# Pinned transposes and a moved projection in a fused attention layer, and joined square roots in the layer after it

## The chip, the core and the metric

The kernel is one program on one core of a Trainium2 chip. The metric is device time in microseconds (us) of one execution, as the median of several runs. A separate, profiled execution gives the trace. The engines are called PE (TensorE, with PEld for its weight loads), DVE (VectorE), ACT (ScalarE), POOL (GpSimd) and SP (which issues most DMAs).

## What is computed

Four layers, each a cross attention and a feed-forward network (FFN), run one after the other on x of shape (4, 256, 256) in float32, with a context of (4, 1601, 256). The change touches the attention of layer 2 and of layer 3 (layers are counted from 0). Cut to these:

```python
# layer 2: 16 query heads, 4 key heads, head size 128
x = layernorm(x)
q, k, v = heads(x @ wq), heads(x @ wk), heads(x @ wv)
q, k = rms_norm(q, q_norm_w), rms_norm(k, k_norm_w)
k_ctx, v_ctx = rms_norm(heads(ctx @ wk_ctx), k_norm_w), heads(ctx @ wv_ctx)
q, k = rotary(q), rotary(k)                      # the context's keys are not rotated
scores = q @ concat(k_ctx, k).T / sqrt(128) + causal_mask_on_the_tokens_part
x = x_in + concat_heads(softmax(scores) @ concat(v_ctx, v)) @ wo
# layer 3: 32 heads of size 8, keys of the context alone
x = layernorm(x)
q, k, v = heads(x @ Wq.T), heads(ctx @ Wk.T), heads(ctx @ Wv.T)
q, k = q * rsqrt(mean(q * q) + 1e-6), k * rsqrt(mean(k * k) + 1e-6)
x = x_in + concat_heads(softmax(q @ k.T / sqrt(8)) @ v)
x = x + quantized_ffn(layernorm(x))              # epsilon of both layer norms: 1e-5
```

## The kernel before

The program is written in a framework with a planner. The Python code gives the instructions in an order (the program order), the planner simulates the engines and puts each engine's instructions into a fixed sequence, in which an instruction that is ready in its simulation may go ahead of earlier ones. On the chip each engine follows that sequence. `tc.keep_in_program_order(ins)` puts `ins` behind the instruction that the code issued before it on the same engine; it holds back nothing else.

**Layer 2** (`l2_xattn`) works through 16 units (batch b, key head g); a unit has four query heads. Keys and values have 15 tiles of 128 rows: 12 of context, one of mixed rows (`CT` = 12), and two of tokens. The score of a query block of 32 is made with the query as weights in four column groups, so a score tile `s2` holds 4 x 32 partitions, and its softmax is made in parts: `scores` gives each partition a maximum `nm` and a sum `sm`, and exponentials `p`; `merge` transposes nm and sm (`ct`, `st`, tile `tm2`) on PE and works out one factor for each partition; `scale` multiplies p by it on POOL; `turn` transposes 32 x 32 blocks on DVE into `pT2`; `values` makes the value products into `o2`, which ACT copies into `at2`; `project` multiplies at by wo into `acc2`, and DVE adds it to x.

The main loop has two steps for each head, so steps 0 to 7 for each unit. In a step the program has scores of two chunks, a step of the softmax of the head before (`soft`), a half of the values of the head before that (`vals`), and then pieces of `prep`, which makes keys, values and queries of the next unit. The first units (`EARLY` = 5) take context keys made earlier from DRAM; the others make them here. The list `WHEN` says how many pieces each step takes; 17 in all for such a unit: two query products, eight pieces of key and value products (tiles 12 and 13; 14; 0 and 1; and so on up to 10 and 11), one that makes the roots and scales (`rstd`, L1031), two with query transposes (`tpqT`, L1048), four with key transposes (`tpk`, L1055). PSUM has two buffers for `s2` and two for the tag `tp`, which tpq, tpkv, tpqT, tpk and acc2 share.

The tokens' keys are rotated into `ko2` (L1024 to L1029) after all products, and scaled on POOL (L1042). The projection of a unit stands in step 3 of the next one, after that step's pieces, when the last values of its head 3 are done.

**Layer 3** works on one batch at a time, in eight groups of four heads. Scores of two context tiles go into two tiles `s3` of three, ACT makes exponentials `e3` (L1532), values follow one pair later. Beside this runs `beside`, a generator that is taken one step further with each pair: keys and values of the next batch (`l3_kv`, 13 tiles, squares, a root, scaling on POOL, transposes), its queries (`queries`) and the FFN of the batch before (`ffn`). Square roots are made on ACT in `rstd` (L72, L73), once for the layer norms of the next and of the previous batch (`norms`), once for the keys, once for the queries.

ACT loads another table (ACT_TABLE_LOAD) where the function changes between the square root and the exponential.

Of the kernel before, what the change touches and what calls it, by code (L numbers as in the profile page):

```python
# [51 lines left out]
class Kernel:  # L52
# [38 lines left out]
    def fill(self, n):  # L91

        for _ in range(n):
            next(self.early, None)
# [771 lines left out]
    def l2_xattn(self):  # L866
# [11 lines left out]
        with ExitStack() as es:  # L878
# [47 lines left out]
            def halves(ap):  # L926
                return ap.rearrange("p h (t d) -> p h t d", t=2)
# [15 lines left out]
            def prep(u, w, ctxT, res):  # L943
# [47 lines left out]
                for ms in ((12, 13), (14,), (0, 1), (2, 3), (4, 5), (6, 7), (8, 9), (10, 11)):  # L991
                    if early and ms[0] < CT:
                        continue
                    tp = ps.tile([P, 2, 256], F32, name="tpkv", tag="tp")
                    rows = P
                    for n, m in enumerate(ms):
                        for k in range(2):
                            if m < CT:
                                self.mm(tp[:, n, :], ctxT[:, k, m * P : (m + 1) * P], w["wkc"][:, k, :], k == 0, k == 1)
                            elif m == CT and early:  # L1000
                                pass
                            elif m == CT:
                                self.mm(tp[:96, n, :], ctxT[:, k, m * P : m * P + 96], w["wkc"][:, k, :], k == 0, k == 1)
                            else:
                                _, t0, rows = OWN[m - 13]
                                self.mm(tp[:rows, n, :], xb[:, k, t0 : t0 + rows], w["wks"][:, k, :], k == 0, k == 1)
                        if m == CT:
                            for k in range(2):
                                self.mm(tp[96:, n, :], xb[:, k, :32], w["wks"][:, k, :], k == 0, k == 1)
                    m, n = ms[0], len(ms)  # L1010
                    if m == CT and early:
                        for t, v in ((kr, tp[:, :, :HD2]), (va, tp[:, :, HD2:])):
                            nc.scalar.copy(t[96:, CT, :], v[96:, 0, :])
                            nc.scalar.copy(t[:, CT + 1, :], v[:, 1, :])
                    else:
                        nc.scalar.copy(kr[:rows, m : m + n, :], tp[:rows, :n, :HD2])
                        nc.scalar.copy(va[:rows, m : m + n, :], tp[:rows, :n, HD2:])
                    if rows < P:
                        nc.gpsimd.memset(kr[rows:, m, :], 0.0)
                    if m in (2, 6, 10, 14):  # L1020
                        squares(CT if m == 14 else m - 2, m + n)
                    yield
                ra, rb = tabs["l2_knw"]
                ko = one.tile([P, 3, HD2], F32, name="ko2")  # L1024
                t2 = one.tile([P, 3, HD2], F32, name="kt2")
                own = kr[:, CT:, :]
                nc.gpsimd.tensor_tensor(ko, own, ra, ALU.mult)
                nc.vector.tensor_tensor(halves(t2), swapped(own), halves(rb), ALU.mult)
                nc.gpsimd.tensor_tensor(ko, ko, t2, ALU.add)  # L1029
                m0 = CT if early else 0  # L1030
# [7 lines left out]
                for m in range(0, 0 if early else CT, 4):  # L1038
                    nc.gpsimd.tensor_tensor(
                        kr[:, m : m + 4, :], kr[:, m : m + 4, :], ss[:, m : m + 4, None].to_broadcast([P, 4, HD2]), ALU.mult  # L1040
                    )
                nc.gpsimd.tensor_tensor(ko, ko, ss[:, CT:NK, None].to_broadcast([P, 3, HD2]), ALU.mult)  # L1042
                yield
                qT = two.tile([P, 4, S], F32, name="qT2")
                for q in range(2):
                    tp = ps.tile([P, 4, P], F32, name="tpqT", tag="tp")
                    for h in range(4):
                        nc.tensor.transpose(tp[:, h, :], qo[q][:, h, :], self.ident)  # L1048
                    nc.scalar.copy(qT[:, :, q * P : (q + 1) * P], tp)
                    yield  # L1050
# [45 lines left out]
            def merge(nm, sm):  # L1096
# [3 lines left out]
                ct, st = t[:8, 0:P], t[:8, P : 2 * P]  # L1100
                nc.tensor.transpose(ct, nm, self.ident)
                nc.tensor.transpose(st, sm, self.ident)
                by = lambda ap: ap.rearrange("n (a j) -> n j a", a=4)
# [43 lines left out]
            def project(hd):  # L1147
                if hd["h"] < 3:
                    return
                b, at, wo = hd["b"], hd["at"], hd["wo"]  # L1150
# [42 lines left out]

            WHEN = [2, 2, 2, 2, 3, 0, 3, 3]
            WHEN_EARLY = [0, 1, 1, 2, 1, 0, 2, 1]
            soft, vals = None, None
            for n, (b, g) in enumerate(units):
                kT, va, qT = ready
                ready, pieces = [], None
                wo_now = wo  # L1200
                at = main.tile([P, 4, S], F32, name="at2", bufs=1)
                for h in range(4):
                    hd = {"nm": self.small.tile([P, 8], F32, name="nm2"), "sm": self.small.tile([P, 8], F32, name="sm2"),
                          "p": [], "va": va, "at": at, "h": h, "b": b, "wo": wo_now}
                    for c in (0, 2):
# [18 lines left out]
                        if pieces is not None:  # L1224
                            for _ in range((WHEN_EARLY if early else WHEN)[step]):
                                next(pieces, None)
                        if vals is not None and c == 2:
                            project(done)
                        if soft is not None and c == 0:
                            next(soft[0])  # L1230
                    done = soft[1] if soft is not None else None
                    vals = value_steps(soft[1]) if soft is not None else None
# [4 lines left out]
            for n in range(2):  # L1237
                next(soft[0])
                next(vals)
                if n == 0:  # L1240
                    next(soft[0])
            project(done)
            for _ in value_steps(soft[1]):
                pass
            project(soft[1])


# [27 lines left out]
    def l3_kv(self, b, st, early):  # L1275
# [6 lines left out]
        va = st["va"] = self.va3[b % 2]  # L1282
        ss = st["ss"] = self.a3.tile([P, (NM + 2) * NH3], F32, name="ss3")
        for m in range(NM):
# [16 lines left out]
            yield  # L1301
        nk = NM * NH3
        self.rstd(ss[:, :nk], ss[:, :nk], 1.0 / HD3, self.eps6)
        for m0, m1 in ((0, 4), (4, 8), (8, 12), (12, NM)):
# [30 lines left out]
    def l3(self, first):  # L1335
# [11 lines left out]
        with ExitStack() as es:  # L1347
# [10 lines left out]
            def bank():  # L1358
                return ps.tile([P, 512], F32, name="b3", tag="tp")

            def norms(bs):

                n = len(bs)
                mv = self.small.tile([P, n, 2, 2], F32, name=f"mv3{n}")
                rs = self.small.tile([P, n, 2], F32, name=f"rs3{n}")
                for t, b in enumerate(bs):
                    st = self.small.tile([P, 2, 6], F32, name="st3")
                    for q in range(2):
                        nc.vector.bn_stats(st[:, q, :], self.x[b][:, q, :])
                        nc.vector.bn_aggr(mv[:, t, q, :], st[:, q, :])  # L1370
                self.rstd(rs, mv[:, :, :, 1], 1.0, self.eps5)
                res = []
                for t, b in enumerate(bs):
                    xn = self.xn.tile([P, 2, D], F32, name="xn3", tag="xn")
                    for q in range(2):
                        nc.vector.tensor_scalar(
                            xn[:, q, :], self.x[b][:, q, :], mv[:, t, q, 0:1], rs[:, t, q : q + 1],
                            ALU.subtract, ALU.mult,
                        )
                    res.append(xn)  # L1380
                return res

            def queries(b, st, xn, fill=lambda n: None):

                ss = st["ss"]
                fill(0)
                tp = bank().rearrange("p (k q t) -> p k q t", k=2, q=2)
# [13 lines left out]
                self.l3_squares(st, qr, NM, True, one)  # L1401
                nk = NM * NH3
                self.rstd(ss[:, nk:], ss[:, nk:], 1.0 / HD3, self.eps6)
                qrv = qr.rearrange("p q (h d) -> p (q h) d", d=HD3)
                nc.vector.tensor_tensor(qrv, qrv, ss[:, nk:, None].to_broadcast([P, 2 * NH3, HD3]), ALU.mult)
                fill(2)
# [154 lines left out]
            def beside(b, st):  # L1561

                if b + 1 < B:
                    kv = st["kv"] if b == 0 else self.l3_kv(b + 1, st, lambda: False)
                    if b:
                        for _ in range(3):
                            next(kv)
                            yield
                    xns = norms([b + 1] + ([b - 1] if b else []))
                    for _ in range(NM - 3 if b else NM - sum(FIRST3)):  # L1570
                        next(kv)
                        yield
                    qs = queries(b + 1, st, xns[0])
                    for _ in range(2):
# [4 lines left out]
                    for _ in qs:  # L1579
                        yield  # L1580
                    old = xns[1:]
                else:
                    for _ in range(3):
                        yield
                    old = norms([b - 1])
                if b == 0:
# [12 lines left out]
            self.l2_add(0)  # L1599
            for _ in queries(0, first, norms([0])[0], lambda n: [next(kv) for _ in range(FIRST3[n])]):  # L1600
                pass
# [44 lines left out]

            xn = norms([B - 1])[0]
            tail = [ffn(B - 1, q, xn, wide) for q in range(2)]
# [157 lines left out]
```

## Time and profile before

| what | value |
|---|---|
| median of 3 runs | 2759.39 us (2759.36 to 2767.87) |
| the profiled execution's own time | 2769.84 us |
| its span, first to last instruction | 2768.1 us |
| mean granted PE clock | 0.979 of full speed |
| busy: PE, PEld, DVE, ACT, POOL | 2630.5, 1483.2, 1354.0, 1245.5, 679.7 us |
| ACT_TABLE_LOAD ahead of a root (L72) | 40, 1283 ns each |
| ACT_TABLE_LOAD ahead of layer 2's exponentials (L1090) | 19 |
| ACT_TABLE_LOAD ahead of layer 3's exponentials (L1532) | 11 |
| POOL, scaling of ko (L1042) | 16, 826 ns each |

A line of a timeline has the start, the length, the engine, the line of the code, the operation, the tile written and the tile read, the shape, the count, and in brackets the time that the engine stood idle before it with the instruction that ended the wait. Matrix products have all one line (L68), since a helper issues them; they are told apart by their tiles. A matrix product of float32 shows as two MATMUL records. The granted clock is the share of full speed at which PE was let run.

### The profile page before, as it was taken

What the parts mean: (1) busy time and instruction counts of PE and PEld (TensorE: products, weight loads), DVE (VectorE), ACT (ScalarE), POOL (GpSimd) and SP (SyncE); (2) the same over time, 40 slices, a digit from 0 to 9 for tenths busy, and PEclk for the clock granted to TensorE, in tenths of its full rate; (3) what the DMA queues carried; (4) which work ended last, traced back from release to release, by engine and by line L of the source; (5) the groups of instructions that cost most, each with busy time, mean ns of one, the idle gap of its engine ahead of it and who ended that gap; (6) DMA issues with size and microseconds to landing.
All of it is one profiled execution on the core that took longest, in us unless ns stands there. A gap on an engine that the chain in (4) does not pass through costs nothing. (4 is left out here: it accounts for less than half of the span.)

```text
span 2768.1 us, 43652 instructions
## 1 busy us (share of the span) xinstructions
PE 2630.5 (95%) x17377; PEld 1483.2 (54%) x17393; DVE 1354.0 (49%) x2604; ACT 1245.5 (45%) x2559; POOL 679.7 (25%) x916
## 2 busy tenths in 40 slices
PE   7999998998999999999999999998999999999997
PEld 4654446444555555555555656555555554544553
DVE  6421126125777766666666666765334323242323
ACT  2321114115444444444444444442325785766775
POOL 1012222214444343333433333432101001001000
PEclk9999999999999999999999999998999999999998
DMA  5133323333110000100001000001322000000000
GB/s 195 58 114 89 89 62 100 88 105 126 38 44 32 20 16 20 41 23 24 13 24 45 16 24 23 2 8 54 141 86 77 18 16 26 4 3 2 6 6 5
DMA packets 57140, 130.10 MB, mean 47 GB/s; under 512 B 7966, under 2 KB 27746, under 8 KB 55914
## 3 DMA queue, kind: packets, MB, share of 16 engines
q1 hardware_dynamic: 54352, 122.94, 13.8%
q8 instruction: 139, 2.28, 0.4%
q0 software_dynamic: 912, 2.49, 0.3%
q10 hardware_dynamic: 1674, 1.88, 0.2%
q14 instruction: 63, 0.52, 0.1%
HBM read 115.14 MB, written 12.14 MB: 46 GB/s over the span
## 5 line engine op out<-in xcount | busy, mean ns | idle before, releaser
L1090 ACT ACTIVATE p<-s,nm 128x448 f32<-128x448 f32 (+1 forms) x512 | 326.7, 644 | 436.2 <-DVE nm L1086 258.1
L1532 ACT ACTIVATE e<-s 128x1024 f32<-128x1024 f32 (+1 forms) x448 | 404.0, 960 | 152.8 <-PE s L68 147.8
L68 PE MATMUL s<-kT,qT 128*32 128x448 f32 (+1 forms) x4096 | 466.0, 566 | 3.9 <-ACT p L1090 3.8
L1126 POOL TENSOR_SCALAR p<-p,rm 128x448 f32<-128x448 f32 (+1 forms) x512 | 322.5, 651 | 554.2 <-DVE rm L1119 333.1
L68 PE MATMUL o<-pT,va 128*128 128x256 f32 (+2 forms) x1920 | 431.9, 376 | 4.4 <-DVE pT L1132 4.2
L68 PEld LDWEIGHTS o<-pT,va 128*128 128x128 f32 (+1 forms) x1920 | 345.5, 191 | 101.7 <-issue 60.2
L1132 DVE STREAM_TRANSPOSE pT<-p 128x896 f32<-128x896 f32 (+1 forms) x256 | 283.2, 1124 | 49.2 <-POOL p L1126 48.3
L68 PE MATMUL s<-qb,kT 32*128 32x256 f32 (+1 forms) x3328 | 272.9, 406 | 18.5 <-ACT e L1532 16.3
L1086 DVE TENSOR_REDUCE nm<-s 128x2 f32<-128x896 f32 (+1 forms) x256 | 282.6, 1105 | 3.5
L68 PEld LDWEIGHTS s<-kT,qT 128*32 128x32 f32 x4096 | 125.2, 111 | 243.7 <-issue 214.9
L68 PE MATMUL o<-e,va 128*32 128x256 f32 (+1 forms) x3328 | 238.2, 394 | 1.2 <-DVE os L1625 1.2
L68 PEld LDWEIGHTS s<-qb,kT 32*128 32x128 f32 (+1 forms) x3328 | 165.8, 182 | 113.1 <-issue 75.8
L68 PEld LDWEIGHTS o<-e,va 128*32 128x32 f32 (+1 forms) x3328 | 91.0, 110 | 115.6 <-issue 75.9
L380 DVE TENSOR_TENSOR f0h<-f0sg,f0u 128x512 f32<-128x512 f32 x48 | 33.0, 687 | 212.4 <-POOL f0sg L378 209.4
L68 PE MATMUL tpkv<-wkc,ctxT 128*128 128x256 f32 (+1 forms) x572 | 130.6, 379 | 0.0
L1559 POOL TENSOR_TENSOR x<-x,t 128x32 f32<-128x32 f32 x64 | 14.7, 250 | 471.9 <-DVE t L1554 471.9
L378 POOL TENSOR_TENSOR f0sg<-f0sg,f0gb 128x512 f32<-128x512 f32 x48 | 60.7, 1266 | 265.9 <-ACT f0sg L376 137.7
L1083 DVE TENSOR_TENSOR s<-s,mask 128x128 f32<-128x128 f32 (+1 forms) x256 | 82.7, 324 | 86.4 <-PE s L68 75.1
L376 ACT ACTIVATE f0sg<-f0g 128x512 f32<-128x512 f32 x48 | 28.7, 597 | 211.0 <-PE f0g L68 207.9
L68 PEld LDWEIGHTS tpkv<-wkc,ctxT 128*128 128x128 f32 (+1 forms) x572 | 107.5, 188 | 15.7
L1090 ACT ACTIVATION_READ_ACCUMULATOR p<-s,nm 128x1 f32 x512 | 100.9, 197 | 0.0
L68 PE MATMUL f0g<-xnT,wg 128*128 128x512 f32 x192 | 90.3, 593 | 0.7 <-ACT f0gT L65 0.7
(417 smaller groups left out, 3399.1 us busy)
## 6 DMA issues: line engine op xcount, KB each, us to landing
ctxT<-in_ctxT SPq DMA_DIRECT2D x10, 1664.0 KB, 8.3
wo<-in_l_wo SPq DMA_DIRECT2D x16, 512.0 KB, 3.6
wq<-in_l_wq SPq DMA_DIRECT2D x16, 512.0 KB, 3.5
f2wgu<-in_l_wgu SPq DMA_DIRECT2D x4, 2048.0 KB, 15.1
ctxn<-in_ctx SPq DMA_DIRECT2D x4, 1664.0 KB, 7.2
f0gb<-f0gd SPq DMA_DIRECT2D x16, 384.0 KB, 4.0
f0gb<-f0gd SPq DMA_DIRECT2D x16, 256.0 KB, 4.3
wks<-in_l_wks SPq DMA_DIRECT2D x16, 256.0 KB, 2.6
```

What stands on the lines that cost most here:

```text
L68: self.nc.tensor.matmul(out, lhsT, rhs, start=start, stop=stop, **kw)
L376: nc.scalar.activation(sg, pgt, AF.Silu)
L378: nc.gpsimd.tensor_tensor(sg, sg, gb[:, tb * 512 : (tb + 1) * 512], ALU.mult)
L380: nc.vector.tensor_tensor(h, sg, pu, ALU.mult)
L1083: nc.vector.tensor_tensor(sv, sv, mask[:, 2 * c : 2 * c + 2, : nt - CT, :].rearrange("p n t i -> p n (t i)"), ALU.add)
L1086: nc.vector.tensor_reduce(nm[:, 2 * c : 2 * c + 2], s[:, :, : nt * 32], AX.X, ALU.max, negate=True)
L1090: nc.scalar.activation(p[:, n, : nt * 32], s[:, n, : nt * 32], AF.Exp, bias=nm[:, e : e + 1], accum_out=sm[:, e : e + 1],)
L1126: nc.gpsimd.tensor_scalar(p[:, n, : nt * 32], p[:, n, : nt * 32], r[:, e : e + 1], 1.0, ALU.mult, ALU.mult)
L1132: nc.vector.transpose(pT[:, 2 * c : 2 * c + 2, :nt, :].rearrange("p n t i -> p n (t i)"), p[:, :, : nt * 32])
L1532: nc.scalar.activation(e[:kr, :, :n, :], s[t][:kr, :, :n, :], AF.Exp, scale=1.0 / math.sqrt(HD3))
L1559: nc.gpsimd.tensor_tensor(xt, xt, t[:, q], ALU.add)
```

## The change

In layer 2:

- the transposes of queries, of maxima and of sums are kept in program order;
- the rotation of the tokens' keys follows tile 14 in the program; its scaling moves from POOL to three activations on ACT;
- the projection of a unit is called in step 5 of the next unit (in step 3 before); for that `at2` has two buffers;
- `WHEN` takes one piece from step 4 to step 3.

In layer 3:

- layer norm statistics of batches 1 to 3 are made at once, at the start of batch 0's work beside;
- for batches 1 to 3 the roots of keys and queries, and the one for the layer norm of the previous batch's FFN, are one activation on one tile `ss3`, which has two more columns; the variance is entered there as 8 var + 8 (1e-5 - 1e-6), so that the root with scale 1/8 and bias 1e-6 gives that of var + 1e-5.

```diff
+                    if m == CT + 2:
+                        ra, rb = tabs["l2_knw"]
+                        ko = one.tile([P, 3, HD2], F32, name="ko2")
...
+                        nc.gpsimd.tensor_tensor(ko, own, ra, ALU.mult)
+                        nc.vector.tensor_tensor(halves(t2), swapped(own), halves(rb), ALU.mult)
+                        nc.gpsimd.tensor_tensor(ko, ko, t2, ALU.add)
                     if m in (2, 6, 10, 14):
                         squares(CT if m == 14 else m - 2, m + n)
                     yield
-                ra, rb = tabs["l2_knw"]
...
-                nc.gpsimd.tensor_tensor(ko, ko, t2, ALU.add)
...
-                nc.gpsimd.tensor_tensor(ko, ko, ss[:, CT:NK, None].to_broadcast([P, 3, HD2]), ALU.mult)
+                for m in range(3):
+                    nc.scalar.activation(ko[:, m, :], ko[:, m, :], AF.Copy, scale=ss[:, CT + m : CT + m + 1])
...
-                        nc.tensor.transpose(tp[:, h, :], qo[q][:, h, :], self.ident)
+                        tc.keep_in_program_order(nc.tensor.transpose(tp[:, h, :], qo[q][:, h, :], self.ident))
...
-                nc.tensor.transpose(ct, nm, self.ident)
-                nc.tensor.transpose(st, sm, self.ident)
+                tc.keep_in_program_order(nc.tensor.transpose(ct, nm, self.ident))
+                tc.keep_in_program_order(nc.tensor.transpose(st, sm, self.ident))
...
-            WHEN = [2, 2, 2, 2, 3, 0, 3, 3]
+            WHEN = [2, 2, 2, 3, 2, 0, 3, 3]
...
-                at = main.tile([P, 4, S], F32, name="at2", bufs=1)
+                at = main.tile([P, 4, S], F32, name="at2", bufs=2)
...
-                        if vals is not None and c == 2:
-                            project(done)
+                        if step == 5 and last is not None:
+                            project(last)
...
-        ss = st["ss"] = self.a3.tile([P, (NM + 2) * NH3], F32, name="ss3")
+        ss = st["ss"] = self.a3.tile([P, (NM + 2) * NH3 + 2], F32, name="ss3")
...
-        self.rstd(ss[:, :nk], ss[:, :nk], 1.0 / HD3, self.eps6)
+        if b == 0:
+            nk = NM * NH3
+            self.rstd(ss[:, :nk], ss[:, :nk], 1.0 / HD3, self.eps6)
...
+                if old is not None:
+                    stats(old)
+                    nc.vector.tensor_scalar(
+                        ss[:, nq:], mv[:, old, :, 1], float(HD3), HD3 * (1e-5 - 1e-6), ALU.mult, ALU.add
+                    )
+                elif b:
+                    nc.vector.memset(ss[:, nq:], 1.0)
+                xn = normed(b, rs[:, b, :])
...
-                self.rstd(ss[:, nk:], ss[:, nk:], 1.0 / HD3, self.eps6)
+                part = ss if b else ss[:, nk:nq]
+                nc.scalar.activation(part, part, AF.Sqrt, bias=self.eps6, scale=1.0 / HD3)
+                nc.vector.reciprocal(ss[:, nk : nq + 2 if b else nq], ss[:, nk : nq + 2 if b else nq])
...
+                if b:
+                    for c in range(0, nk, nk // 2):
+                        nc.vector.reciprocal(ss[:, c : c + nk // 2], ss[:, c : c + nk // 2])
...
-                    xns = norms([b + 1] + ([b - 1] if b else []))
+                    if b == 0:
+                        norms(range(1, B))
...
-                    qs = queries(b + 1, st, xns[0])
+                    qs = queries(b + 1, st, b - 1 if b else None)
...
-                    old = xns[1:]
+                    nq = (NM + 2) * NH3
+                    old = [normed(b - 1, st["ss"][:, nq:])] if b else []
```

Here `stats(b)` makes the layer norm statistics of one batch into `mv`, `normed(b, r)` subtracts the mean and multiplies by r, and `norms` does the statistics and one root for several batches. `nq` is the column behind the queries' sums.

## The prediction

> **What bounds the kernel now.** I read the profile in the order: busy time of each engine by stretch, who waits for whom on TensorE, timelines of the places named there. By the timelines, layer 2's attention runs from 658 to 1926 us (its units with keys made in the unit before, "full" units, from 950 on) and layer 3's from 2127 to 2742 us. Columns: stretch and its length, busy PE, PEld, DVE, ACT and POOL, granted clock, DMA:
>
> ```profile
> core 0: us, PE busy (x) PEld busy (x) DVE busy (x) ACT busy (x) POOL busy (x), PEclk, DMA share, GB/s
> 950.00:1905.00 955.00, 918.34 (x5735) 554.55 (x5734) 635.94 (x1048) 439.76 (x1183) 352.29 (x492) 0.99 0.07 21
> 2127.00:2742.00 615.00, 590.70 (x7105) 309.49 (x7118) 192.04 (x463) 445.24 (x497) 47.45 (x83) 0.98 0.04 12
> ```
>
> TensorE is busy 96% in both, the next engine 67% and 72%. Time can come only from PE's idle 36.7 and 24.3 us, and from clock that is not granted. The waits of PE in the first stretch (total us, times, longest):
>
> ```profile
> PE tpqT L1048 <- POOL qo L1035: 21.7, 22, 1.9
> PE tm L1102 <- ACT p L1090: 9.1, 12, 0.8
> PE tpk L1055 <- ACT kT L1057: 4.4, 11, 0.4
> ```
>
> These are the same three places in each of 11 units, as PE's timeline of one shows (start, length, what, idle before):
>
> ```profile
> 1314.91 3.29 PE L68 MATMUL o<-pT,va 128*128 128x256 f32 x14
> 1319.80 0.66 PE L1048 MATMUL tpqT<-ident,qo 128*128 128x128 f32 x4 [1.60 <-POOL qo L1035]
> 1320.80 0.66 PE L1048 MATMUL tpqT<-ident,qo 128*128 128x128 f32 x4 [0.34 <-POOL qo L1035]
> 1321.38 3.21 PE L68 MATMUL s<-kT,qT 128*32 128x448 f32 x32
> ...
> 1336.09 1.04 PE L1055 MATMUL tpk<-ident,kr 128*128 128x128 f32 x8
> 1336.97 0.27 PE L1101 MATMUL tm<-ident,nm 128*8 128x128 f32 x1
> 1338.02 0.27 PE L1102 MATMUL tm<-ident,sm 128*8 128x128 f32 x1 [0.78 <-ACT p L1090]
> 1338.68 0.52 PE L1055 MATMUL tpk<-ident,ko 128*128 128x128 f32 x3 [0.40 <-ACT kT L1057]
> ```
>
> The program writes the query transposes behind the score and value products of step 6; here they stand ahead of those scores (1321.38), where POOL is still scaling qo. The planner put them forward. Likewise the maxima's transposes (tm) stand ahead of the next unit's first scores.
>
> Layer 3 has one large wait, for exponentials, where ACT does a square root between two table loads:
>
> ```profile
> PE s L68 <- ACT e L1532: 16.3, 8, 2.6
> ```
>
> ```profile
> 2326.88 1.28 ACT L72 ACT_TABLE_LOAD   x1
> 2330.41 0.64 ACT L72 ACTIVATE ss<-ss,eps 128x416 f32<-128x416 f32 x1 [2.24 <-DVE ss L1330]
> 2331.07 1.28 ACT L1532 ACT_TABLE_LOAD   x1
> ```
>
> PE's next scores then come at 2333.43, after 2.61 idle. The eight waits: keys' roots 2.40, 2.61, 2.61; queries' roots 2.30 three times; norms 0.26 and 1.49.
>
> A wait costs more than its idle time. Two stretches with the same query stall:
>
> ```profile
> 984.00:990.00 6.00, 5.66 (x40) 2.14 (x40) 2.99 (x4) 2.78 (x9) 3.63 (x4) 0.72 0.01 3
> 1318.00:1324.00 6.00, 4.05 (x37) 1.77 (x40) 4.57 (x6) 4.67 (x12) 5.42 (x6) 1.00 0.01 3
> ```
>
> In the first the clock fell (0.72 over 6 us: 1.7 us lost), in the second not. Going through both layers in stretches of 2 us, I find six such falls in the full units, all behind a query stall, 1.7 each, **10.2 us**; in layer 3 they sum to **13.6 us**, all behind a root's wait.
>
> **What the Trainium skill says.** "TensorE: Matmul & The Clock Gate", section "Part 1: The HAM clock gate", says an idle PE falls to half clock and needs a busy window of about 3.4 us to recover, the window running freely. The trace agrees on the loss (half of 3.4 is the 1.7 seen) and on the chance in it (6 of 11 equal stalls), but 2 us of idle is enough here. "ScalarE: Activation LUTs", section "What ACT_TABLE_LOAD costs", gives 1.28 us a load plus 1.38 of drain; the trace has the 1.28, and the exponential starts right behind it. "PSUM — Partial Sum Buffer", section "Engine vs sequencer instructions": matmuls start in program order; so an early transpose holds all scores behind it, as above.
>
> **The change, part by part.**
>
> *Layer 2, pinned transposes.* tpqT goes behind step 6's 32 scores, two tm and 16 value products, 3.2+0.3+3.4 = 6.9 us of PE work. qo is ready at 1320.7; the transposes now could start at 1318.1. What is late next? The scores of step 6, which come forward into the gap: their first buffer is free only when the exponentials of step 5 have read it, 1319.97, the second at 1322.05 (ACT's timeline). That would put a stall of 1.8 in place of the 1.94. But the projection moves to step 5 (16 matmuls, 3.7 us in the trace at 1379.99; one DVE add of 0.69; no DMA), ahead of exactly these scores: first scores at about 1321.9, second half 1323.5. Cover holds by 1.9 and 1.4. So **-21.7** (bounds -21.7 and 0, if the projection lands elsewhere).
>
> *Clock.* Without a 2 us gap the six falls should go: -10.2; I leave one: **-8** (bounds -10.2 and 0).
>
> *Unit's end.* tm pinned behind the scores takes its wait of 0.78 away, but the third tpk there waits for a bank that ACT's kT copy at 1337.85 frees, and that copy stands behind the exponentials (until 1337.85). PE now waits for it from 1337.1 to about 1338.6: 1.4 for 1.18, as 0.25 of tm's work has left the gap. 11 x 0.25 = **+3** (bounds -13.5, if the planner finds filler, and +8, if the longer gap makes half of the units fall in clock at 1.7). tm runs some 5 us later at step 0; its reader on PE (L1117) today waits for query products till 1349.1 while DVE had it ready at 1341.4, so that costs nothing. Elsewhere tm already stands behind the scores.
>
> *Tokens' keys.* The two POOL and one DVE instruction of the rotation come earlier in the program, but in the trace all 16 already run straight behind ACT's copy of kr (1360.05): 0. On POOL 0.83 us a unit goes; POOL is 37% busy: 0. On ACT three 128x128 copies with a scale come in, not in the trace; the skill's price (the ScalarE section above: 186+0.83N ns, 93 a pointer, 93 overlapped) gives an estimate of 0.29 each; the trace's 128x512 kin takes 0.69, which that formula gives too. 0.9 us a unit, at ACT's busiest point, between the root and step 5's exponentials. Queued behind: those exponentials, and PE's step-6 scores behind them; the margins of 1.9 and 1.4 above cover it: **0** (bounds 0 and 11 x 0.9 = +10).
>
> *WHEN.* One key product (8 matmuls, 1.8 us, two copies) moves from step 4 to 3; a second buffer for at lets the projection wait two steps. PE work is the same: 0. No step moved past a queue issues a DMA; SP's loads stay where they are.
>
> Layer 2: -21.7 - 8 + 3 = **-27**.
>
> *Layer 3.* The keys' roots join the queries', and norms are made once for three batches. Idle gone: 2.40+2.61+2.61+0.26 = 7.9. Each remaining joint root is 482 wide: 0.70 for 0.35, +0.35 x 3 = +1.0. Clock: at three remaining stalls 1.7 to 2.5 of the 13.6 stay each, so -6 to -8.5; I take -6. Added DVE work (statistics 1.1 us, two halves of the keys' reciprocal in place of one of 2.75) meets a DVE 31% busy: 0. The keys' scaling on POOL comes later: joint root at 2341 (query product) + 5.4, reciprocals and products of 0.55+0.69+1.4, POOL 1.96: first keys at 2351; the first key transposes stand at 2355, so 4 us of slack: 0 (bounds 0 and +2 a batch). Three batches: -7.9 + 1.0 - 6 = **-13** (bounds -18 and -4).
>
> **Sum:** -40. The profiled execution took 2769.84 (span 2768.1), 10.4 above the median 2759.39, so it would be 2730. The runs shown differ by 8.5, the size of five clock falls (an estimate); a median with fewer falls has less to win from the clock: of its 14 I count 8 there. 2759.4 - 26 - 8 = **2725**.
>
> **Rivals.**
> *A, exponentials take over* (15%): step 6's scores wait for ACT because the planner puts the projection elsewhere or the three copies ahead of the exponentials. For: ACT's free buffer at 1319.97 and 1322.05, close to the old start. Against: 3.7 us of projection. Layer 2 then gives only some clock, layer 3 its 13: about 2744.
> *B, slower, the unit's end* (9%): ACT's copies of ko fall behind step 7's exponentials, just ahead of the kT copies. Then PE stands 1.4+0.9 waiting for ko's product, and as much again for its copy, with the clock down two windows (3.4): about 6 to 7 us for 1.18 in each of 11 units, +60 against the -40 that is won elsewhere: 2775. It decides from 4 us a unit. Against: ko is ready 20 us earlier.
> *C, nothing moves* (6%): the planner finds other work to put forward into the same waits; layer 3's gain is eaten by longer joint roots: 2756.
>
> **How the numbers follow.** The forecast has 70%: 2706 to 2740, from the clock's and the unit's end's bounds. 0.3% is 8.3 us, about what a measurement of this kernel can tell from no change: below 2751 is faster. Forecast and A are faster, 0.85; C the same, 0.06; B slower, 0.09. The range takes the forecast and A with its bounds: 2705 to 2750.
>
> **What would show it.** Right: tpqT's wait for qo gone, transposes behind step 6's values; acc between step 5's values and step 6's scores; few clock falls in 950 to 1905; in layer 3 five roots for ten among the exponentials and 8 to 9 us of waits for e, not 16.3. Wrong: a new "s <- ACT p" of over 10 us in layer 2 (A), "tpk <- ACT" above 30 us (B), or a layer 3 that waits for key transposes.

## The result and the profile after

| | before | after |
|---|---|---|
| median, runs on the same chip | 2761.94 us (4 runs) | 2726.32 us (2722.96 to 2728.46, 4 runs) |
| ratio to before | 1 | 0.9867, 95% interval [0.9845, 0.9888] |
| profiled execution, its span | 2769.84, 2768.1 us | 2727.83, 2726.1 us |
| layer 2, first to last score product | 658.3 to 1897.3: 1239.0 us | 654.6 to 1863.4: 1208.8 us |
| layer 3, first to last score product | 2127.5 to 2737.0: 609.5 us | 2096.5 to 2694.6: 598.1 us |

The kernel is 35.6 us faster by the medians. In the profiled pair the span falls by 42.0: layer 2 gives 30.2, layer 3 gives 11.4, and the stretches around them the other 0.4 (3.7 won ahead of layer 2, where no code changed, 2.9 lost between the layers, 0.4 lost at the end).

Who waits for whom on TensorE after the change, in the full units (950 to 1900 us; total us, times, longest; the other waits in this view lie past the last scores):

```profile
PE tpk L1057 <- ACT kT L1059: 16.1, 11, 1.5
PE tm L1104 <- ACT p L1092: 0.6, 1, 0.6
```

The largest entry of before, tpqT for POOL's qo, is gone, and so is tm's wait; the one tm wait left lies past the last scores. What is left at the unit's end is one wait of 1.47 us (16.1 / 11). The same view for the units in front of them (640 to 950 us), where the maxima of the first unit are now late:

```profile
PE s L68 <- ACT p L1092: 7.2, 5, 3.0
PE o L68 <- DVE pT L1134: 3.2, 1, 3.2
PE s L68 <- ACT kT L1062: 1.3, 1, 1.3
```

They sum to 11.7 us. In the kernel before the same stretch has 9.4, of which 1.3 are tpqT's:

```profile
PE s L68 <- ACT p L1090: 3.8, 2, 3.0
PE tm L1101 <- DVE nm L1086: 1.9, 1, 1.9
PE o L68 <- DVE pT L1132: 1.5, 1, 1.5
PE tpqT L1048 <- POOL qo L1035: 1.3, 2, 0.9
PE tm L1102 <- ACT p L1090: 0.9, 1, 0.9
```

PE's timeline of a full unit (start, length, what, idle before in brackets):

```profile
1299.32 3.29 PE L68 MATMUL o<-pT,va 128*128 128x256 f32 x14
1302.45 3.62 PE L68 MATMUL acc<-wo,at 128*128 128x256 f32 x16
1305.99 3.21 PE L68 MATMUL s<-kT,qT 128*32 128x448 f32 x32
1309.14 0.27 PE L1103 MATMUL tm<-ident,nm 128*8 128x128 f32 x1
...
1309.36 3.36 PE L68 MATMUL o<-pT,va 128*128 128x256 f32 x16
1312.56 1.04 PE L1050 MATMUL tpqT<-ident,qo 128*128 128x128 f32 x8
...
1321.66 1.04 PE L1057 MATMUL tpk<-ident,kr 128*128 128x128 f32 x8
1324.16 0.55 PE L1057 MATMUL tpk<-ident,ko 128*128 128x128 f32 x3 [1.47 <-ACT kT L1059]
```

The projection (acc) fills the time between step 5's values and step 6's scores, and those scores start at 1305.99 without a wait. The eight query transposes stand behind step 6's values, in one group of 1.04 us and not in two of 0.66. The only bracket is the one at the unit's end.

Layer 3: the wait for exponentials, and a joint root of keys and queries on ACT's timeline with the gap it makes on PE's:

```profile
PE s L68 <- ACT e L1549: 11.0, 4, 3.4
```

```profile
2304.44 1.28 ACT L1416 ACT_TABLE_LOAD   x1 [0.80 <-DVE ss L1330]
2305.74 0.70 ACT L1416 ACTIVATE ss<-ss,eps 128x482 f32<-128x482 f32 x1
2306.45 1.28 ACT L1549 ACT_TABLE_LOAD   x1
```

```profile
2308.82 2.08 PE L68 MATMUL s<-qb,kT 32*128 32x256 f32 x8 [3.43 <-ACT e L1549]
```

Four waits are left of eight, and five roots of ten between the first and the last score product. The root takes the 0.70 of the forecast, but its table load starts 0.80 after ACT is free, and PE stands 3.43 us.

Two other waits of PE came with the new layer 3. The first line is before, the other two are after:

```profile
PE b L68 <- DVE va L1292: 1.6, 3, 0.9
PE b L68 <- DVE va L1291: 2.6, 3, 1.9
PE fill L68 <- ACT va L1291: 2.3, 1, 2.3
```

The wait of 1.88 us (0.90 before) ends at 2102.77: on DVE's timeline the statistics of three batches, begun at 2099.46, now stand ahead of the copy into va at 2102.17. The wait of 2.32 ends at 2081.52, ahead of layer 3, and is new: on ACT the first layer norm's root stands ahead of the copies into va and waits 4.48 us for DVE's `mv`. Why DVE makes `mv` later there is not shown. All nine kernels of this document with the new layer 3 have waits of 1.88 and of 2.3 to 2.4 at these places, and the four with the old one have 0.9 and none. The 2.32 is most of what is lost between the layers.

The two layers by stretch, in the columns of before (stretch and its length, busy PE, PEld, DVE, ACT and POOL, granted clock, DMA):

```profile
654.60:1863.40 1208.80, 1180.35 (x7533) 702.08 (x7534) 844.39 (x1409) 585.47 (x1602) 454.09 (x637) 0.99 0.08 25
2096.50:2694.60 598.10, 580.25 (x7074) 304.42 (x7090) 196.51 (x459) 427.75 (x477) 48.19 (x81) 0.98 0.04 12
```

Between the same two score products the kernel before has PE busy for 1194.03 of 1239.00 and 587.34 of 609.50. So in layer 2 idle falls from 45.0 to 28.5 us (-16.5) and busy time, for the same work, by 13.7; in layer 3 idle falls from 22.2 to 17.9 (-4.3) and busy time by 7.1.

### The profile page after: what moved, and what is told of

It reads as the page before. It is cut to its first block, busy times and chain, and to the rows that moved or that the text cites. A ratio compares the mean times of both kernels' runs of the same rounds, so it can differ in the third digit from the quotient of the medians.

```text
span 2726.1 us, 43670 instructions
## 1 busy us (share of the span) xinstructions
PE 2607.7 (96%) x17377; PEld 1478.8 (54%) x17393; DVE 1355.9 (50%) x2608; ACT 1245.8 (46%) x2592; POOL 671.0 (25%) x900
## 3 DMA queue, kind: packets, MB, share of 16 engines
q10 hardware_dynamic: 1674, 1.88, 0.2%
## 5 line engine op out<-in xcount | busy, mean ns | idle before, releaser
L68 PE MATMUL s<-kT,qT 128*32 128x448 f32 (+1 forms) x4096 | 457.6, 560 | 8.7 <-ACT p L1092 7.2
## 6 DMA issues: line engine op xcount, KB each, us to landing
f2wgu<-in_l_wgu SPq DMA_DIRECT2D x4, 2048.0 KB, 13.7
```

The lines of the kernel that those rows point to most:

```text
L68: self.nc.tensor.matmul(out, lhsT, rhs, start=start, stop=stop, **kw)
```

## The experiments

My theory was the sum of the prediction: layer 2 gains by the query wait and the clock behind it, layer 3 by joining roots. The open questions were whether the two parts add, which of layer 2's edits does the work (pins, projection, rotation, schedule), and what the two new or grown waits cost. Ratios are to the kernel before, with 95% intervals; "us" is the median's distance from before in the same comparison.

**The two halves alone.** Layer 2 alone has the new code of layer 2 with the old code of layer 3; layer 3 alone is the reverse.

```
layer 2 alone:  the changed kernel up to l3_open, the kernel before from there on
layer 3 alone:  the kernel before up to l3_open, the changed kernel from there on
```

> Layer 2 changed, layer 3 as before. The theory (layer 2 wins by the stalls of its query transposes and the clock behind them): 25 to 32 us below before, ratio 0.988 to 0.991, no wait of tpqT for qo, and a wait of tpk for kT of about 1.5 in each of 11 units. The rival (most of the gain is in layer 3): 5 to 12 us below, ratio above 0.995.

> Layer 3 changed, layer 2 as before. The theory: 9 to 14 us below before, ratio 0.995 to 0.997, waits of scores for exponentials 11 in place of 16.3 us. The rival (layer 3 carries the gain): over 25 us below, ratio under 0.991.

Measured: layer 2 alone 2733.35 us, 0.9902 [0.9882, 0.9921], -28.5; layer 3 alone 2754.34 us, 0.9974 [0.9963, 0.9985], -7.5. The sum is -36.0, the whole change -35.6: the halves add, and neither uses up what the other wins. Layer 2 came out as expected; layer 3 stayed short of its 9 to 14, and its trace has the new and grown waits that are shown above.

**The projection back in step 3, pins kept.** This asks whether the pinned transposes or the projection win layer 2's time.

```
-                        if step == 5 and last is not None:
+                        if step == 3 and last is not None:
                             project(last)
```

> The changed kernel with the projection back in step 3; the pins stay. The theory (the projection covers ACT's root before the scores of step 6, and the pins alone gain little): these scores wait for exponentials about 1.8 us in each full unit, some 20 us in all with clock falls behind some of them, so 20 to 30 us above the changed kernel, ratio 0.994 to 0.998. The rival (the pins are what wins): as the changed kernel, 0.987, and no such wait.

Measured: 2770.93 us, 1.0029 [1.0018, 1.0040], slower than before, 44 us above the changed kernel where 20 to 30 were expected. The waits of PE from 940 to 1900 us, and its timeline at one of them:

```profile
PE s L68 <- ACT p L1092: 26.5, 11, 2.8
PE tpk L1057 <- ACT kT L1059: 16.1, 11, 1.5
```

```profile
988.36 3.21 PE L68 MATMUL s<-kT,qT 128*32 128x448 f32 x32 [1.36 <-ACT p L1092]
...
1403.30 3.29 PE L68 MATMUL o<-pT,va 128*128 128x256 f32 x14
1409.39 4.91 PE L68 MATMUL s<-kT,qT 128*32 128x448 f32 x32 [2.80 <-ACT p L1092]
```

ACT's timeline at the second of these waits has the three activations on ko at the place where the exponentials of step 5 are made:

```profile
1407.73 0.97 ACT L1044 ACTIVATE ko<-ko,ss 128x128 f32<-128x128 f32 x3
```

Without the 3.6 us of projection ahead of them, step 6's scores come before ACT has emptied their buffers. The wait is 2.80 us in eight units and 1.36 in three, and the 32 products behind the one shown last 4.91 us in place of 3.21: the clock fell. Over the full units 13.6 us of clock are lost, a fall of 1.7 behind each of the eight longer waits and none behind the three shorter ones. The 2.80 is 1.0 more than was forecast for this case; the three activations, 0.97 us, stand between the first exponential (1407.07) and the second (1408.60), and the scores start right behind the second. So rival A's mechanism is real, with both of its reasons in it; 26.5 + 13.6 = 40 of the 44 us are these waits and their clock. The pins win nothing in this kernel. Pins alone, with ko still scaled on POOL, were not run.

**The projection alone.** The kernel before with `project` at step 5 and two buffers for `at`; nothing pinned, the old rotation, the old schedule, the old layer 3.

```
-                if hd["h"] < 3:
-                    return
-                at = main.tile([P, 4, S], F32, name="at2", bufs=1)
+                at = main.tile([P, 4, S], F32, name="at2", bufs=2)
-                        if vals is not None and c == 2:
-                            project(done)
+                        if step == 5 and last is not None:
+                            project(last)
```

> The kernel before with nothing but the projection in step 5 and the second buffer for at; no pin, layer 3 as before. In the built sequence the query transposes now stand behind the values of step 6 although nothing pins them. The theory (with the projection there the planner has no gap to fill and puts no transpose forward): 27 to 33 us below before, ratio 0.988 to 0.990, no wait of tpqT for qo, unit's end as before at 0.78 and 0.40. The rival (pins are needed): 0.997 or more, with the wait of 21.7 kept.

Measured: 2724.48 us, 0.9866 [0.9843, 0.9888], -37.4: as much as the whole change, from one edit of layer 2, and more than the 27 to 33 expected. Layer 2 alone, measured beside it, was never below 2729.14 us, and this kernel never above 2728.59: the rest of the new layer 2 costs time. Its waits from 940 to 1900 us, and PE's timeline of a full unit:

```profile
PE tm L1102 <- ACT p L1090: 9.1, 12, 0.8
PE tpk L1055 <- ACT kT L1057: 4.4, 11, 0.4
```

```profile
1298.41 3.36 PE L68 MATMUL o<-pT,va 128*128 128x256 f32 x16
1301.61 1.04 PE L1048 MATMUL tpqT<-ident,qo 128*128 128x128 f32 x8
...
1311.59 0.27 PE L1101 MATMUL tm<-ident,nm 128*8 128x128 f32 x1
1312.64 0.27 PE L1102 MATMUL tm<-ident,sm 128*8 128x128 f32 x1 [0.78 <-ACT p L1090]
1313.31 0.52 PE L1055 MATMUL tpk<-ident,ko 128*128 128x128 f32 x3 [0.40 <-ACT kT L1057]
```

The query transposes stand behind step 6's values with no pin to hold them there, and no tpqT wait is left in the full units. With the projection ahead of step 6's scores the planner no longer puts the transposes in front of them. That it is the closed gap that keeps it from doing so is argued: acc2 and tpqT also share the two buffers of the tag tp, and no run closes the gap with work that takes none of them. The unit's end is that of before, 0.78 + 0.40.

**The pins taken out, and put in.** Two tests from opposite sides: the changed kernel without any pin, and the projection alone with all of them.

```
no pins:              - tc.keep_in_program_order(nc.tensor.transpose(ct, nm, self.ident))
                      + nc.tensor.transpose(ct, nm, self.ident)        (st and tpqT likewise)
projection and pins:  the same three lines the other way, in the kernel of the experiment above
```

> The changed kernel without its pins (queries', maxima's and sums' transposes free), all else kept. In the full units the built sequence of TensorE differs from the changed kernel's only at the unit's end (the two tm stand ahead of tpk of ko); in the first units transposes go forward into the waits for exponentials. The theory (the pins cost, the projection wins): unit's end 13.5 us of waits in place of 16.1, and 3 to 6 us less in the first units with their clock: 5 to 9 us below the changed kernel, ratio 0.984 to 0.985. The rival (what separates the changed layer 2 from the projection alone is the move of ko to ACT or of the key product): as the changed kernel, 0.987.

> The kernel before with the projection at step 5, two buffers for at, and the transposes of queries and maxima pinned in program order; schedule, rotation of the tokens' keys and layer 3 as before. Projection alone gave 0.9866, the whole of the new layer 2 0.9902. Theory (the pins are what costs those 10 us, by waits that the planner may no longer fill): ratio 0.990, 2734 us, 'tpk <- ACT kT' 15 to 17 us with the wait of tm gone. Rival (the pins cost nothing, and the moved key product or the moved rotation costs it, or it is scatter of the clock): 0.9866, 2724 us.

Measured: no pins 2720.86 us, 0.9853 [0.9831, 0.9876], against 0.9867 with them; projection and pins 2730.37 us, 0.9890 [0.9871, 0.9909], against 0.9866 without. Taking them out is 3.9 us better (0.0014 x 2760), putting them in 6.6 worse (0.0024 x 2760). Each pair's intervals overlap, and both pairs point the same way. The gain without pins stayed below the 5 to 9 us expected. Beside the kernel without pins two others were measured that keep them, those of the next two experiments: its five times lie between 2716.91 and 2721.94, their ten between 2722.20 and 2728.09. The waits say where it is. Projection and pins, from 640 to 950 and then from 940 to 1900 us:

```profile
PE s L68 <- ACT p L1090: 9.4, 4, 3.5
PE o L68 <- DVE pT L1132: 3.2, 1, 3.2
PE s L68 <- ACT kT L1060: 1.3, 1, 1.3
```

```profile
PE tpk L1055 <- ACT kT L1057: 17.2, 11, 1.6
```

At the unit's end 17.2 stand in place of 9.1 + 4.4, +3.7. In the units in front the three waits sum to 13.9; in the projection alone five waits there sum to 8.8. There the pinned tm and tpqT can no longer be put into the first unit's gaps. Together that is +8.8 of idle, for some 6.6 us of time. Over all kernels of this document the waits in front sum to 11.7 to 13.9 where the transposes are pinned and to 8.1 to 9.4 where they are not; with the projection in step 5 the unit's end has 16.1 to 17.3 with pins and 12.6 to 13.6 without. The rotation and the schedule were not tested singly. Together they make no difference that could be told: the kernel without pins (2720.86, 2716.91 to 2721.94) has both, and the first of the two kernels at the end of this section (2717.82, 2712.34 to 2720.57) has neither, and besides scales ko on POOL and makes the variances on ACT.

**The scaling of ko back on POOL.**

```
-                for m in range(3):
-                    nc.scalar.activation(ko[:, m, :], ko[:, m, :], AF.Copy, scale=ss[:, CT + m : CT + m + 1])
+                nc.gpsimd.tensor_tensor(ko, ko, ss[:, CT:NK, None].to_broadcast([P, 3, HD2]), ALU.mult)
```

> The changed kernel with the tokens' keys scaled on POOL in one instruction again. The theory (three activations of about 0.97 us together lie inside ACT's margin ahead of the scores of step 6): no difference from the changed kernel, within 3 us, ratio 0.986 to 0.988. The rival (they delay the exponentials that the scores wait for): 5 to 10 us below the changed kernel, ratio under 0.985.

Measured: 2724.04 us, 0.9870 [0.9848, 0.9892], against 0.9867. The three activations last 0.97 us on ACT's timeline (1303.75 to 1304.72), between the first and the second of step 5's four exponentials, and nothing is won by taking them away: the projection covers them, as the forecast had it.

**The variance scaled on ACT in layer 3.** In the changed kernel the joint root of batches 2 and 3 waits for two engines, DVE and POOL. In the instruction sequence the table load carries the wait for DVE and the root the one for POOL, and in the trace the load starts when DVE has made the queries' sums (`ss`, L1330). In batch 1, where no variances are joined, the root waits for DVE alone and the load ahead of it for nothing. This kernel makes the variances on ACT itself, and that earlier activation takes the wait for POOL.

```
-                    nc.vector.tensor_scalar(
-                        ss[:, nq:], mv[:, old, :, 1], float(HD3), HD3 * (1e-5 - 1e-6), ALU.mult, ALU.add
-                    )
+                    nc.scalar.activation(
+                        ss[:, nq:], mv[:, old, :, 1], AF.Copy, bias=HD3 * (1e-5 - 1e-6), scale=float(HD3)
+                    )
```

> The changed kernel with the two variance columns written by an activation on ACT in place of a DVE instruction, so that the joint root of batches 2 and 3 waits for one engine in place of two (the wait for POOL is taken at the earlier activation), and its table load no longer carries the wait for DVE. The theory (the 3.43 us waits hold 0.8 us of a table load that waits for the sums): the two waits fall to about 2.65, 1.6 us less in all, up to 5 with clock falls; ratio 0.985 to 0.987. The rival (the load starts no earlier, or the wait comes from the wider root): waits stay at 3.4.

Measured: 2727.98 us, 0.9874 [0.9852, 0.9897]. ACT's timeline at the same root, and the wait for exponentials:

```profile
2303.48 0.63 ACT L1327 ACTIVATE sqq<-qr 128x512 f32<-128x512 f32 x1 [1.66 <-DVE qr L1413]
2304.13 1.28 ACT L1416 ACT_TABLE_LOAD   x1
2305.43 0.70 ACT L1416 ACTIVATE ss<-ss,eps 128x482 f32<-128x482 f32 x1
```

```profile
PE s L68 <- ACT e L1549: 9.4, 4, 2.7
```

The load now starts right behind the square, and the waits fall from 11.0 to 9.4. That shows the cause of the longer wait. The lost clock of layer 3 stays at 12.0 us. 1.6 us are too few for the median to show: the ratio can't be told from 0.9867.

**An earlier piece at the unit's end.** In the changed kernel one more piece of key work goes to step 6, one fewer to step 7, so that the last transposes have a bank before the wait.

```
-            WHEN = [2, 2, 2, 3, 2, 0, 3, 3]
+            WHEN = [2, 2, 2, 3, 2, 0, 4, 2]
```

> The changed kernel with the schedule WHEN at [2, 2, 2, 3, 2, 0, 4, 2] in place of [2, 2, 2, 3, 2, 0, 3, 3]: one more piece at step 6, one fewer at step 7, so that the last key transposes of a unit have a bank before the exponentials hold up ACT's copies. Theory (the wait 'tpk <- ACT kT' of 16.1 us at the unit's end is a gap on the path): it falls below 5 us, nothing takes its place, and the kernel gains some 11 us on the changed one: 2715, ratio to before 0.983. Rival (the next unit's first scores wait for the same copies of kT and qT anyway): the wait reappears as 's <- ACT kT' or 's <- ACT qT' of 10 us or more and the time stays at 2726, ratio 0.987.

Measured: 2728.61 us, 0.9884 [0.9865, 0.9902]; no gain. My theory fell. The waits from 940 to 1900 us:

```profile
PE tpq L68 <- ACT kT L1059: 12.6, 8, 1.6
PE tp_ln L918 <- ACT kT L1059: 3.1, 2, 1.6
PE acc L68 <- ACT kT L1059: 1.6, 1, 1.6
```

```profile
1323.71 0.49 PE L1057 MATMUL tpk<-ident,ko 128*128 128x128 f32 x3
1325.77 1.13 PE L68 MATMUL tpq<-wq,xT 128*128 128x512 f32 x2 [1.57 <-ACT kT L1059]
```

ko's transposes no longer wait, and the next product that wants a bank of the same ring does, for the same copies of ACT behind the exponentials: 17.3 us in place of 16.1. The rival had named this, though at the next scores.

**What the parts suggest.** The first of these two has the projection alone and the new layer 3 with the variance on ACT; the second adds the earlier piece.

```
projection and roots:  layer 2 of the projection alone + the new layer 3 with the variance on ACT
with earlier piece:    the same, WHEN = [2, 2, 2, 2, 3, 0, 4, 2]
```

> Layer 2 of the kernel before with nothing but the projection moved, and the changed layer 3 with the variance on ACT. The theory (the parts add): 37 us from the projection, 7.5 from the joined roots, 1.6 to 5 from the table load: 45 to 50 us below before, ratio 0.982 to 0.984, faster than both kernels. The rival (the gains overlap, since both come out of the same clock): as the projection alone, 0.9866.

> The kernel before with three things: layer 2's projection at step 5 with two buffers for at, WHEN at [2, 2, 2, 2, 3, 0, 4, 2], and the new layer 3 with the variance scaled on ACT; no pins, rotation of the tokens' keys where it was. Theory: the same as projection and roots together (0.9842 measured), less the unit's end of 9.1 + 4.4 us, of which about 10 go: 2708 us, ratio 0.981. Rival (a gap at the unit's end is filled by something else that waits): 0.984 as without the new schedule.

Measured: 2717.82 us, 0.9842 [0.9819, 0.9865], and 2716.14 us, 0.9839 [0.9822, 0.9857]. The first is at -42.2, short of the 45 to 50 expected but below the projection alone, so most of both gains adds up; it is some 7 us below the changed kernel by the ratios (0.0025 x 2760), though the intervals overlap. The second was expected at 2708: the earlier piece adds nothing here either, as its rival had it; its waits at the unit's end sum to 13.6 (tm 10.3, the rest behind kT copies), against 13.5. Both medians are the lowest of this study, with the pins, the moved rotation and the change's own schedule left out.

## Why the prediction was right, point by point

Forecast 2725, measured 2726. The waits that were named did go, but that the sum came within 1 us is luck: the terms miss in both directions. Against the profiled pair, which fell by 42.0 where the sum had 40:

| term | forecast | measured |
|---|---|---|
| tpqT's wait in layer 2 | -21.7 | -21.7 in the full units, -1.3 in front |
| layer 2's clock | -8 | -3.4: lost in the full units 10.2 to 0, in front 0 to 6.8 |
| unit's end | +3 | 13.5 to 16.1: +2.6 |
| ko on ACT | 0 | 0 |
| waits of the first unit | not priced | +3.6 (8.1 to 11.7) |
| tpqT in one group | not priced | busy 19.47 to 15.55: -3.9 |
| layer 2, the rest of busy time | not priced | -6.4 (-13.7 without the -3.4 and the -3.9), not explained |
| layer 3, idle | -7.9 + 1.0 | -4.3 |
| layer 3, clock | -6 | granted clock some -2 of busy -7.1 |
| between the layers | not priced | +2.9 |

**"Layer 2, pinned transposes": right in size, and wrong in what earned it.** The prediction put -21.7 on the pins and gave the projection the part of cover, with 0 as the bound "if the projection lands elsewhere". The projection alone (0.9866) and the projection elsewhere (1.0029) show that it does both: it covers the wait of step 6's scores, and with it in place the transposes no longer go forward. The cause, that the planner fills a gap that it sees ahead of those scores, was in the prediction; that the cover takes away the gap, and with it the need for a pin, I didn't draw from it.

**Layer 2's clock: right in the full units, missed in front.** All six falls are gone, and none of the ten kernels with the projection in step 5 has one there. In front the longer waits of the first unit brought new ones, 6.8 us of lost clock in this profile. That part is partly chance: profiles of the same layer 2 have 1.7 to 6.8 there, and those of the layer 2 of before 0 and 3.4.

**"Elsewhere tm already stands behind the scores": wrong.** In the first unit, which has little work beside it, tm and tpqT did fill gaps before, and the pins take that away, +3.6 us here. It didn't show in the sum because the query transposes take 0.28 us less in one group (1.04 against 0.66 + 0.66), in each of 15 units.

**Unit's end: right.** Forecast 1.4 for 1.18 a unit, measured 1.47, with no fall of clock behind it. (The upper bound of +8 was too low by its own terms: 3 + 5.5 x 1.7 is 12.) Its cover was gone, and nothing else was late.

**Layer 3's idle time: two costs were missed.** By its terms PE's gaps were to be 2.65 each (2.30 + 0.35); measured are 2.65 in batch 1, then 3.43 twice, because the table load of batches 2 and 3 waits for DVE's sums (shown by making the variances on ACT). The prediction priced the joint root by its width alone. And "added DVE work" was put at 0 because DVE is 31% busy: DVE had time, but the statistics stood ahead of a copy into va that PE waited for, +1.0. The two costs, 1.6 and 1.0, are the difference between -6.9 and -4.3. The wait of 2.32 ahead of layer 3 was not foreseen either. The sign "8 to 9 us of waits for e" was also less than its own terms give: 16.3 - 7.9 + 1.0 is 9.4, what the kernel with the variance on ACT has.

**Layer 3's clock: the roots' part near the forecast, two falls elsewhere.** Lost clock, in stretches of 2 us, falls from 13.6 to 12.0, by some 2 where 6 was forecast. All 13.6 stood behind roots' waits; behind the three joint roots 8.5 are left (1.7 and twice 3.4), 5 less. The other 3.4 are two falls that were not there before: one behind the wait for va that grew to 1.88, one behind a wait for `os` of 1.25 that is as long as before. Yet PE's busy time for the same products falls by 7.1. The records of granted clock explain no more than 3 of it; where the other 4 come from no run here tells.

**The rivals.** A's waits are what the projection in step 3 shows, and they cost more than A had. B's unit with ko late didn't occur: ko is scaled 20 us ahead of its transposes. C's planner found nothing else to put forward in the full units.

## What to carry to other kernels

Where an automatic order puts an instruction too early, ask first what gap it was filling: close the gap with useful work, and the order may come right by itself, while a pin also forbids the places where filling helped. A wait for a bank of a ring moves with the next user of the ring, so an earlier slot for one user won nothing here, where the reader that frees the bank came no earlier. And where two small operations are joined into one, count every engine the joint one now waits for.

## What the runs showed of the hardware

**Length of a gap and fall of clock.** The Trainium skill, "TensorE: Matmul & The Clock Gate", section "Part 1: The HAM clock gate", puts the fall behind an idle window of about 3.4 us that runs freely. The runs show falls behind shorter gaps, and in layer 2 more of them the longer the gap is:

| kernel | repeated gap in the full units, us | falls of 1.7 us |
|---|---|---|
| projection in step 3, three units | 1.36 | none of 3 |
| after; with the earlier piece; projection and pins | 1.47; 1.57; 1.56 | none of 11 in each |
| before | 1.60 + 0.34 | 6 of 11 |
| projection in step 3, eight units | 2.80 | 8 of 8 |

So in these units 1.57 us was free of it, 2 us brought it in about half, and 2.80 always. The length of the gap does not decide alone: in layer 3 a wait for `os` of 1.25 us has a fall of 1.7 or 3.4 behind it in all nine kernels with the new layer 3, and none in the four with the old one. What makes the difference is open.

**VectorE beside POOL.** While POOL scales kr (2308.51 to 2315.28), the same DVE operation takes three times as long as just after:

```profile
2313.46 1.33 DVE L1373 TENSOR_SCALAR xn<-x,mv,rs 128x256 f32<-128x256 f32 x1
2315.81 0.40 DVE L1373 TENSOR_SCALAR xn<-x,mv,rs 128x256 f32<-128x256 f32 x1
```

In the kernel before, the sixteen operations of this line in layer 3's part take 0.40 to 0.41 us, and none of them falls beside this scaling. This DVE work is off the path here. That the two engines hinder each other is argued from the times alone; no run takes POOL's work away.
